# Dense attention of a four-layer network: scores laid out by keys instead of by queries

## The chip, the cores and the metric

The kernel runs on one core of one Trainium2 chip. The metric is the device time of one execution in microseconds (us). The core has five engines that run side by side: TensorE (PE in the profile; its weight loads are shown apart as PEld), VectorE (DVE), ScalarE (ACT), GpSimd (POOL) and SyncE (SP, which issues most transfers). Matrix products are written to eight PSUM banks of 128 partitions and 512 f32 columns; everything else lives in SBUF.

## The reference

The network works on x of 4 batches, 1024 positions and 128 features, in this order: a feed-forward layer, an attention by distances with 16 heads, the feed-forward layer again, a local attention with gated layer, the dense causal attention that this document is about, and the local layer again. What the change touches is the dense attention, 16 heads of 64 features (cut):

```python
xn = (x - mu) / jnp.sqrt(var + 1e-05) * ln_gamma + ln_beta
qkv = jnp.einsum('bnd,ed->bne', xn, w_qkv)
...
q, k, v = (reshape(q) * scale, reshape(k), reshape(v))
sim = jnp.einsum('bhid,bhjd->bhij', q, k)
sim = jnp.where(causal, mask_value, sim)
sim = sim - jax.lax.stop_gradient(jnp.max(sim, axis=-1, keepdims=True))
attn = jax.nn.softmax(sim, axis=-1)
out = jnp.einsum('bhij,bhjd->bhid', attn, v)
out = out.transpose(0, 2, 1, 3).reshape(b, n, INNER)
return jnp.einsum('bne,de->bnd', out, w_out) + b_out
```

The result is added to x.

## The kernel before

**A planner sets the order.** Every piece of work is a small Python function, a step, that is filed with `at(t, f)` under a due time. The steps run once as a recording: each instruction is priced by `cost` (L285), and which step reads or writes which buffer is noted. `order` (L352) then plays the steps through a model of the five engines and of the buffers, takes on each engine the ready step that is most urgent, and `best_order` (L563) repeats this six times, with urgencies taken from the play before, and keeps the shortest. The real instructions are issued in that order, and `follow` (L221) ties each engine to it. So the order on each engine is fixed when the kernel is built, by the prices in `cost`, over all six layers at once. All instructions are issued by one helper, which is why the profile puts them all on line 237. Buffers come from a few large tensors: `wordsP` is PSUM, `wordsS` and `wordsR` are SBUF areas for the whole run (of `WORDS` and `ROUNDED` words a partition, the second for the rounded type fp32r), and `words` is an area of `SWING` words that is given from layer to layer.

For an f32 matmul the price of TensorE is (L292 to L298)

```python
            x, w = args[2], args[1]
            if x.dtype == F32:
                t = 4 * free_size(x) / 2400
```

where `x` is the streaming operand and `w` the weights; 0.004 us are added.

**The dense attention** is `attn1` (L1087). It works through 32 head pairs `n` (4 batches of 8 pairs; a pair is 2 heads of 64 features, 128 rows in all), one every `T` microseconds of due time. For each pair, `project` (L1204) makes queries and keys, features on the partitions and positions in the columns, each split into a rounded high part and a low part so that two passes of the rounded type give the precision of f32 (tiles `q`, `k` and `kz`); `value` (L1255) makes the values with positions on the partitions; `norm` (L1149) does the LayerNorm of the next batch, one tile of 128 positions beside each pair.

`heads` (L1273) then takes a tile `i` of 128 queries. `score` (L1279) puts queries on the partitions and up to 512 keys in the columns of a PSUM bank (banks 0 to 3), two passes with the queries as weights, and adds the causal mask to the diagonal tile by a bf16 matmul. `top` and `top2` take the negated maximum of each row on VectorE, `exp` takes the exponential on ScalarE straight from PSUM with the maximum as its bias and sums each row in its accumulator, `inverse` takes the reciprocal of the sum, and `normalise` (L1316) multiplies the row by it on GpSimd. `turn` (L1320) turns each 128 x 128 tile of exponentials on TensorE, 72 a pair, into banks 4 and 5, and `keep` (L1328) copies them out, two of three on ScalarE and the third on VectorE. `weigh` (L1350) takes two tiles of queries together: for each tile of keys and each head, 64 value columns are the weights, 256 turned exponentials stream, and the two heads write partitions 0 to 63 and 64 to 127 of bank 6. `output`, `project_out` and `collect` add the bias, project and add to x, through bank 7, which projections and values use as well.

Of the kernel before, what the change touches and what calls it, by code (L numbers as in the profile page):

```python
# [19 lines left out]
S = 1024  # L20
# [5 lines left out]
BANKS, ROUNDED, SWING, WORDS = 4096, 14208, 10240, 28744  # L26
# [65 lines left out]
class Plan:  # L92
# [222 lines left out]
    def prepare(self):  # L315
# [25 lines left out]
        for g in self.used_tags:  # L341
            for slot in g.slots:
                for c in slot:
                    c.tags[g] = True

# [6 lines left out]
    def order(self):  # L352
# [69 lines left out]
        def take(s, found):  # L422
            for (t, slot), b in zip(found, s.buffers):
                b.slot, b.lo = slot, slot[0].lo
                for c in slot:
                    c.free = False
                    s.behind += [c.held] if c.held is not None else [x for h in b.tag.before[c] for x in h.buffers]
                b.tag.next += 1
            for b in s.buffers:
                for g in b.slot[0].tags:  # L430
                    wake(g)
# [163 lines left out]
class Macaron:  # L595
# [491 lines left out]
    def attn1(self, ph, T0, lead):  # L1087
# [4 lines left out]
        T = 30.9  # L1092
# [56 lines left out]
        def norm(t0, w, b, t):  # L1149
# [13 lines left out]

            def scale():
                mv, v, y = V[K]
                V["xn", K] = tile_([128, D], "xn", 3)
                ve.tensor_scalar(V["xn", K], x(), mv[:, 0:1], y, ALU.subtract, ALU.mult)
# [20 lines left out]
            self.rsqrt(V, tile_, [t0 + (0.2 + 0.1 * j) * w for j in range(8)], lambda: V[K][1:], K + ("r",))  # L1188
# [8 lines left out]
        low_key = lambda j: plan.tile([128, 512], f"a1.kz{j}", R, FR, swing=True, kept=True)  # L1197
# [55 lines left out]


        def value(t0, b, g, t):  # L1255
            ks = slice(128 * (t % 4), 128 * (t % 4) + 128)

            def start():
                V["v", b, g, t] = tile_([128, 512], f"v{g}{t}")
                h, l = V["h", b, t // 4]  # L1260
                ps = V["pv", b, g, t] = wide()
                pe.matmul(ps, h[:, ks], W["h", 4 + g], start=True, stop=False)
                pe.matmul(ps, h[:, ks], W["l", 4 + g], start=False, stop=False)
                pe.matmul(ps, l[:, ks], W["h", 4 + g], start=False, stop=True)

            def keep():
                ve.tensor_copy(V["v", b, g, t], V["pv", b, g, t])

            at(t0, start)
            at(t0 + 0.8, keep)  # L1270


        def heads(t0, n, i):  # L1273
            TK = 128 * (i + 1)
            parts = [slice(c, min(TK, c + 512)) for c in range(0, TK, 512)]
            two = len(parts) == 2
            K = (n, i)

            def score(z, k):  # L1279
                ks = parts[z]  # L1280
                w = ks.stop - ks.start
                dg = ks.stop == TK
                if z == 0:
                    V["m", K, k] = tile_([128, 3], "nm", 8), tile_([128, 3], "su", 8), tile_([128, 1], "rc", 8)
                q1, k1, kz = V["q", n, i // 4], V["k", n, z], V["kz", n, z]
                qs, ks = slice(128 * (i % 4), 128 * (i % 4) + 128), slice(0, w)
                sc = V["s", K, k, z] = plan.bank("a1.s", [0, 1, 2, 3])
                pe.matmul(sc[:, 0:w], q1[k][:, qs], k1[k][:, ks], start=True, stop=False)
                pe.matmul(sc[:, 0:w], q1[k][:, qs], kz[k][:, ks], start=False, stop=not dg)
                if dg:  # L1290
                    pe.matmul(sc[:, w - 128 : w], self.identb, W["cm"], start=False, stop=True)

            def top(z, k):
                o = V["m", K, k][0][:, z : z + 1]
                ve.tensor_reduce(o, V["s", K, k, z][:, 0 : parts[z].stop - parts[z].start], AX.X, ALU.max, negate=True)

            def top2(k):
                nm = V["m", K, k][0]
                ve.tensor_reduce(nm[:, 2:3], nm[:, 0:2], AX.X, ALU.min)

            def exp(z, k):
                nm, su, _ = V["m", K, k]
                if z == 0:
                    V["e", K, k] = tile_([128, S], "e", 4)
                sc = V["s", K, k, z][:, 0 : parts[z].stop - parts[z].start]
                c = 2 if two else 0
                ac.activation(V["e", K, k][:, parts[z]], sc, AF.Exp, bias=nm[:, c : c + 1], accum_out=su[:, z : z + 1])

            def inverse(k):
                _, su, rc = V["m", K, k]  # L1310
                if two:
                    ve.tensor_reduce(su[:, 2:3], su[:, 0:2], AX.X, ALU.add)
                c = 2 if two else 0
                ve.reciprocal(rc, su[:, c : c + 1])

            def normalise(k):  # L1316
                e = V["e", K, k][:, 0:TK]
                gp.tensor_scalar(e, e, V["m", K, k][2], 1.0, ALU.mult, ALU.mult)

            def turn(k, c):  # L1320
                m = min(4, i + 1 - 4 * c)
                if i % 2 == 0:
                    V["et", n, i // 2, k, c] = tile_([128, 4, 2, 128], "et", 6)
                pt = V["t", K, k, c] = plan.bank("a1.t", [4, 5], (128, 4, 128))
                for j in range(m):
                    pe.transpose(pt[:, j, :], V["e", K, k][:, 128 * (4 * c + j) : 128 * (4 * c + j) + 128], self.ident)

            def keep(k, c, dve):  # L1328
                m = min(4, i + 1 - 4 * c)
                E = ("et", n, i // 2, k, c)  # L1330
                put = ve.tensor_copy if dve else ac.copy
                put(V[E][:, 0:m, i % 2, :], V["t", K, k, c][:, 0:m, :])

            for z in range(len(parts)):
                for k in range(2):
                    at(t0 + 0.45 * z + 0.9 * k, score, z, k)
                    at(t0 + 0.9 * z + 0.9 + 0.1 * k, top, z, k)
                    at(t0 + 2.2 + 0.1 * k + 0.5 * z, exp, z, k)
            for k in range(2):
                if two:  # L1340
                    at(t0 + 2.1 + 0.1 * k, top2, k)
                at(t0 + 3.5 + 0.1 * k, inverse, k)
                at(t0 + 3.6 + 0.1 * k, normalise, k)
                for c in range((i + 4) // 4):
                    at(t0 + 5.0 + 0.1 * k + 0.2 * c, turn, k, c)
                    self.turns = self.turns + 1
                    at(t0 + 5.5 + 0.1 * k + 0.2 * c, keep, k, c, self.turns % 3 == 0)


        def weigh(t0, n, i2):  # L1350
            b, p = divmod(n, 8)
            h = i2 // 2

            def products():
                if i2 % 2 == 0:
                    V["po", n, h] = plan.bank("a1.o", [6])
                po, c = V["po", n, h], 128 * (p % 4)
                c0 = 256 * (i2 % 2)
                for j in range(2 * i2 + 2):
                    u = 128 if j == 2 * i2 + 1 else 0  # L1360
                    for k in range(2):
                        pe.matmul(
                            po[64 * k : 64 * k + 64, c0 + u : c0 + 256],
                            V["v", b, p // 4, j][:, c + 64 * k : c + 64 * k + 64],
                            V["et", n, i2, k, j // 4][:, j % 4].rearrange("p u s -> p (u s)")[:, u:256],
                            start=(j == 0),
                            stop=(j == 2 * i2 + 1),
                            skip_group_check=True,
                        )

            def output():
                V["oT", n, h] = tile_([128, 512], "oT", 2)
                ac.activation(V["oT", n, h], V["po", n, h], AF.Identity, bias=W["bias"][:, 16 + p : 17 + p])
# [11 lines left out]
            at(t0, products)  # L1385
            if i2 % 2:
                at(t0 + 3.5, output)
                at(t0 + 4.5, project_out)
                at(t0 + 5.5, collect)
# [4 lines left out]
        self.turns = 0  # L1394
# [12 lines left out]
        work = [2 * (3.3 * (i + 1) + 2) for i in range(8)]  # L1407
        for n in range(N):
# [11 lines left out]
            for i in range(8):  # L1420
                ti = t0 + T * sum(work[:i]) / sum(work)
                heads(ti, n, i)
                if i % 2:
                    weigh(ti + 7.0 + 0.15 * i, n, i // 2)
# [576 lines left out]
def tile_macaron(ctx: ExitStack, tc: tile.TileContext, a: dict, out: bass.AP, phases=PHASES):  # L2001
# [3 lines left out]
    for k, ph in enumerate(phases):  # L2005
# [3 lines left out]
        elif ph == "attn0":  # L2009
            t = m.attn0(ph, t + 3.0, 46.0)  # L2010
        elif ph == "attn1":
            t = m.attn1(ph, t + 3.0, 40.0)
        else:
            t = m.ffn1(ph, t + 3.0, k == len(phases) - 1)
# [71 lines left out]
```

## Time and profile before

| what | value |
|---|---|
| median of the runs shown | 3249.35 us (3249.25 to 3252.34) |
| the profiled execution | 3244.27 us, of which 3242.3 us are the span from first to last instruction |
| mean granted TensorE clock | 0.984 |
| busy over the span: PE, PEld | 3033.2 us (94%), 2128.3 us (66%) |
| busy over the span: DVE, ACT, POOL | 2237.5 us (69%), 2455.6 us (76%), 1461.8 us (45%) |
| the dense attention in the trace | about 1430 to 2510 us |

How to read it. A line of a group has the engine, the operation, output and inputs by tile names, for matmuls the weights as rows*columns and then the streaming operand as partitions x columns, the type, the number of instructions, their busy time and the mean length of one in ns, and the idle time before them with what ended it. Matmuls are pipelined: the recorded lengths of neighbours overlap, so the cost of one in a stream is the distance between starts and not its length. A line of a timeline has start and length in us of a run of equal instructions.

### The profile page before, as it was taken

The numbers are of one execution on the slowest core, as the hardware profiler recorded it, in microseconds if no ns is written. First come the engines' busy times: TensorE is split into PE (matmuls) and PEld (weight loads), VectorE is DVE, ScalarE is ACT, GpSimd is POOL, SyncE is SP. The second block draws the span as 40 slices with busy tenths as digits, with TensorE's granted clock in tenths as the row PEclk, the third lists the DMA queues.
The fourth block names the chain that finished last, engine by engine and source line by source line (L and its number), as shares of the span: only waits on it lengthen the run. The fifth ranks groups of instructions, "written<-read, shape, count | busy, mean of one in ns | idle before, by whom it ended". The sixth has DMA issues, their size and how long they took to land.

```text
span 3242.3 us, 76442 instructions
## 1 busy us (share of the span) xinstructions
PE 3033.2 (94%) x27033; PEld 2128.3 (66%) x27060; DVE 2237.5 (69%) x6889; ACT 2455.6 (76%) x6818; POOL 1461.8 (45%) x1627
## 2 busy tenths in 40 slices
PE   8999999989998999889999999999999899999988
PEld 6322222667776777667777777777777677777767
DVE  8433341568767676788888888887787787676774
ACT  6999999778868686647767766777777788686873
POOL 1000000179958585433333333333343799585870
PEclk9999999999999999989999999999999999999999
DMA  1000000022212121222222121222231322122211
GB/s 40 1 1 1 1 3 11 25 69 64 55 39 59 44 56 31 52 67 46 47 52 45 42 51 42 45 48 52 45 84 35 75 56 58 37 59 46 57 42 30
DMA packets 212596, 138.96 MB, mean 43 GB/s; under 512 B 148516, under 2 KB 167800, under 8 KB 212216
## 3 DMA queue, kind: packets, MB, share of 16 engines
q1 hardware_dynamic: 211496, 133.51, 18.1%
q8 instruction: 217, 3.56, 0.5%
q14 instruction: 163, 1.34, 0.1%
q0 software_dynamic: 720, 0.56, 0.1%
HBM read 19.22 MB, written 2.10 MB: 7 GB/s over the span
## 4 chain that ended last, share of the span: by engine, by line
PE 54%; DVE 17%; ACT 17%; issue 6%; POOL 5%; DMA 1%; SPq 1%; DVEq 0%; ACTq 0%; POOLq 0%
PE wordsP L237 54%; ACT wordsS L237 12%; DVE wordsS L237 11%; DVE words L237 4%; POOL wordsS L237 4%; ACT words L237 4%; POOL words L237 1%; DVE wordsP L237 1%; DVE wordsR L237 1%; SPq L237 1%; ACT wordsR L237 0%; DMA wordsS<-wordsS 0%; ACT wordsP L237 0%; DMA words<-W_vT 0%; DMA words<-words 0%
## 5 line engine op out<-in xcount | busy, mean ns | idle before, releaser
L237 PE MATMUL wordsP<-wordsS 128*128 128x128 f32 (+7 forms) x12013 | 1653.3, 330 | 131.6 <-POOL wordsS L237 48.7
L237 ACT ACTIVATE wordsS<-wordsP,wordsS 128x128 f32<-128x128 f32 (+4 forms) x1952 | 920.8, 495 | 349.8 <-PE wordsP L237 211.0
L237 PEld LDWEIGHTS wordsP<-wordsS 128*128 128x128 f32 (+3 forms) x10248 | 916.2, 144 | 356.2 <-POOL wordsS L237 101.8
L237 POOL TENSOR_SCALAR wordsS<-wordsS 128x128 f32<-128x128 f32 (+7 forms) x630 | 478.0, 761 | 686.3 <-DVE wordsS L237 489.0
L237 PE MATMUL wordsP<-wordsR 128*128 128x512 f32 (+2 forms) x2592 | 725.9, 411 | 20.1 <-DVE wordsR L237 5.9
L237 POOL TENSOR_TENSOR wordsS<-wordsS 128x512 f32<-128x512 f32 (+1 forms) x518 | 541.5, 1060 | 445.4 <-DVE wordsS L237 422.1
L237 ACT COPY wordsS<-wordsP 128x512 f32<-128x512 f32 (+4 forms) x1040 | 543.2, 540 | 188.1 <-PE wordsP L237 181.0
L237 DVE TENSOR_REDUCE wordsS<-wordsP 128x1 f32<-128x512 f32 (+4 forms) x1024 | 576.4, 581 | 75.3 <-PE wordsP L237 68.8
L237 PE MATMUL wordsP<-wordsS,words 128*64 128x64 f32 (+3 forms) x6216 | 521.3, 298 | 32.3 <-DVE words L237 12.6
L237 PEld LDWEIGHTS wordsP<-wordsR 128*128 128x128 f32 (+1 forms) x2592 | 454.7, 192 | 124.0 <-ACT words L237 10.2
L237 ACT ACTIVATE wordsS<-wordsP 128x1024 f32<-128x1024 f32 (+3 forms) x640 | 515.7, 869 | 25.1 <-PE wordsP L237 20.7
L237 PE MATMUL wordsP<-words 128*128 128x512 f32 (+3 forms) x1540 | 418.1, 376 | 11.9 <-DMA words<-W_vT 10.6
L237 ACT ACTIVATION_READ_ACCUMULATOR wordsS<-wordsP,wordsS 128x1 f32 x1792 | 397.5, 222 | 0.0
L237 DVE COPY wordsS<-wordsP 128x512 f32<-128x512 f32 (+4 forms) x444 | 238.6, 550 | 211.0 <-PE wordsP L237 206.2
L237 PEld LDWEIGHTS <-wordsS 64*128 64x128 bf16 (+1 forms) x1792 | 117.9, 95 | 389.3 <-issue 372.2
L237 PEld LDWEIGHTS wordsP<-wordsS,words 128*64 128x64 f32 (+2 forms) x5704 | 300.4, 136 | 99.1 <-issue 47.5
L237 DVE TENSOR_TENSOR wordsS<-wordsP,wordsS 128x256 f32<-128x256 f32 (+3 forms) x560 | 251.9, 461 | 160.7 <-PE wordsP L237 123.1
L237 DVE TENSOR_TENSOR words<-wordsP,wordsS 128x256 f32<-128x256 f32 (+1 forms) x448 | 227.3, 526 | 129.8 <-PE wordsP L237 83.9
L237 PEld LDWEIGHTS wordsP<-words 128*128 128x128 f32 x1540 | 247.7, 192 | 43.4 <-DMA words<-W_kT 10.6
L237 PEld LDWEIGHTS wordsP<-words,wordsS 64*64 64x64 f32 (+1 forms) x4672 | 186.6, 142 | 78.3 <-issue 54.6
L237 PE MATMUL wordsP<-words,wordsS 64*64 64x128 f32 (+1 forms) x4672 | 227.2, 279 | 7.7 <-POOL words L237 2.7
L237 ACT ACTIVATE words<-wordsP,wordsS 128x512 fp32r<-128x512 f32 (+1 forms) x192 | 131.2, 690 | 73.3 <-PE wordsP L237 66.3
(62 smaller groups left out, 2263.7 us busy)
## 6 DMA issues: line engine op xcount, KB each, us to landing
words<-words SPq DMA_DIRECT2D x648, 128.0 KB
wordsS<-words SPq DMA_DIRECT2D x88, 128.0 KB
wordsS<-wordsS SPq DMA_DIRECT2D x48, 128.0 KB
wordsS<-wordsS SPq DMA_DIRECT2D x48, 112.0 KB
wordsS<-c_rot SPq DMA_DIRECT2D x16, 256.0 KB
wordsS<-L_attn_x SPq DMA_DIRECT2D x8, 256.0 KB
words<-wordsS SPq DMA_DIRECT2D x16, 128.0 KB
out_dram<-wordsS SPq DMA_DIRECT2D x8, 256.0 KB
```

Source lines behind the costliest of these rows:

```text
L237: self.follow(engine, getattr(engine.engine, name)(*args, **kw))
```

## The change

The scores are laid out the other way round. `heads` goes, and `block` takes 512 queries of one head: for each tile `j` of 128 keys it puts the keys on the partitions and the queries in the columns (the keys are now the weights, the queries stream). ScalarE copies each such tile from PSUM to SBUF, and VectorE keeps a running maximum `M` over the tiles, 128 x 512. `M` is turned on TensorE, reduced by VectorE to one maximum for each query, spread again over all partitions by a second turn of a broadcast column, and copied out by ScalarE as `B`. GpSimd subtracts `B` from the stored scores, and ScalarE takes the exponential in place. These tiles already have keys on the partitions, so they go into `weigh` as the weights, in tiles of 128 x 128, and the values stream, with a 65th column of ones whose product is the sum of the exponentials. `divide` divides by it on VectorE, and only the output (four tiles of 128 x 128 for 512 queries of a pair) is turned, for the projection. Beside that: the LayerNorm scales on ScalarE and its root is written out in small VectorE steps; a woken planner step may also be one that waits for a tag sharing the place (`peers`); the low keys move from the swinging area to the rounded one; `T`, area sizes and one due time change; the tile of ones is filled by GpSimd for the first batch.

```diff
-BANKS, ROUNDED, SWING, WORDS = 4096, 14208, 10240, 28744
+BANKS, ROUNDED, SWING, WORDS = 4096, 14208, 7168, 31816
...
+        for g in self.used_tags:
+            g.peers = {h: True for slot in g.slots for c in slot for h in c.tags}
...
-                for g in b.slot[0].tags:
+                for g in b.tag.peers:
                     wake(g)
...
-        T = 30.9
+        T = 29.0
...
             def scale():
-                mv, v, y = V[K]
                 V["xn", K] = tile_([128, D], "xn", 3)
-                ve.tensor_scalar(V["xn", K], x(), mv[:, 0:1], y, ALU.subtract, ALU.mult)
+                ac.activation(V["xn", K], x(), AF.Identity, bias=V["rt", K], scale=V[K][2])
...
-        low_key = lambda j: plan.tile([128, 512], f"a1.kz{j}", R, FR, swing=True, kept=True)
+        low_key = lambda j: plan.tile([128, 512], f"a1.kz{j}", R, FR, kept=True)
...
+        ones = lambda g, t: tile_([128, 8, 65], f"v{g}{t}", 1, F32, False, True)
...
-        def heads(t0, n, i):
...
+        def block(t0, w, n, h, k):
+            K = (n, h, k)
+            b, p = divmod(n, 8)
+            J = 4 * h + 4
+
+            first = [max(0, j - 4 * h) for j in range(J)]
+            groups = [range(j, j + 2) for j in range(0, 4 * h, 2)] + [range(4 * h + z, 4 * h + z + 1 + z // 2) for z in range(3)]
...
+            def score(j):
...
+                ks, c = slice(128 * (j % 4), 128 * (j % 4) + 128), 128 * first[j]
+                q1, k1, kz = V["q", n, h][k][:, c:512], V["k", n, j // 4][k][:, ks], V["kz", n, j // 4][k][:, ks]
+                sc = V["s", K, j] = plan.bank("a1.s", [0, 1, 2])[:, 0 : 512 - c]
+                dg = j >= 4 * h
+                pe.matmul(sc, k1, q1, start=True, stop=False)
+                pe.matmul(sc, kz, q1, start=False, stop=not dg)
                 if dg:
...
+                    pe.matmul(sc[:, 0:128], W["cm"], self.identb, start=False, stop=True)
+
+            def store(j):
+                ac.copy(part([j]), V["s", K, j])
+
+            def top(j):
...
+                ve.tensor_tensor(V["M", K][:, c:512], V["s", K, j], other, ALU.max)
+
+            def turn():
+                pt = V["t", K] = plan.bank("a1.t", [3, 4], (128, 4, 128))
+                for u in range(4):
+                    x = part([0])[:, 0:128] if h == u == 0 else V["M", K][:, 128 * u : 128 * u + 128]
+                    pe.transpose(pt[:, u, :], x, self.ident)
+
+            def top2():
+                V["m", K] = tile_([128, 4], "nm", 3)
+                ve.tensor_reduce(V["m", K], V["t", K], AX.X, ALU.max)
+
+            def spread():
+                pt = V["tb", K] = plan.bank("a1.t", [3, 4], (128, 4, 128))
+                for u in range(4):
+                    pe.transpose(pt[:, u, :], V["m", K][:, u : u + 1].broadcast_to([128, 128]), self.ident)
+
+            def keep():
+                V["B", K] = tile_([128, 4, 128], "B", 3)
+                ac.copy(V["B", K], V["tb", K])
+
+            def shift(q):
+                x, y = part(q), flat(V["B", K])[:, 128 * first[q[0]] : 512]
...
+                gp.tensor_tensor(x, x, y, ALU.subtract)
+
+            def exp(q):
+                ac.activation(part(q), part(q), AF.Exp)
+
+            def weigh(j):
+                if j == 0:
+                    V["po", K] = plan.bank("a1.o", [5, 6])[:, 0:260].rearrange("p (u k) -> p u k", k=65)
+                v = V["v", b, p // 4, j][:, 2 * (p % 4) + k, :]
+                for u in range(first[j], 4):
+                    e = part([j])[:, 128 * (u - first[j]) : 128 * (u - first[j]) + 128]
+
+                    pe.matmul(V["po", K][:, u, :], e, v, start=(j == u == 0), stop=(j == 4 * h + u), skip_group_check=True)
+
+            def divide():
...
+                ve.reciprocal(rc, po[:, :, 64])
+                o = V["on", n, h][:, :, 64 * k : 64 * k + 64]
+                ve.tensor_tensor(o, po[:, :, 0:64], rc.unsqueeze(2).broadcast_to([128, 4, 64]), ALU.mult)
+
+            def turn_o():
+                pt = V["ot", n, h] = wide()
+                for u in range(4):
+                    pe.transpose(pt[:, 128 * u : 128 * u + 128], V["on", n, h][:, u, :], self.ident)
...
-        work = [2 * (3.3 * (i + 1) + 2) for i in range(8)]
+        work = [0.14, 0.14, 0.36, 0.36]
...
+            for j, (h, k) in enumerate(((0, 0), (0, 1), (1, 0), (1, 1))):
+                block(t0 + T * sum(work[:j]), T * work[j], n, h, k)
...
-            t = m.ffn1(ph, t + 3.0, k == len(phases) - 1)
+            t = m.ffn1(ph, t + (3.0 if k < 4 else 8.0), k == len(phases) - 1)
```

More of the change, by code (lines that the diff above doesn't have):

```diff
@@ L1162, in var, with root @@
                 ve.tensor_scalar(v, mv[:, 1:2], 1.0 + EPS, EPS * EPS, ALU.mult, ALU.add)
+            def root(j):
+                mv, v, y = V[K]
+                if j == 0:
+                    V["rt", K] = tile_([128, 1], "rt1", 3)
+                    ve.tensor_scalar(y.bitcast(I32), v.bitcast(I32), -0.5, float(0x5F3759DF), ALU.mult, ALU.add)
+                    return
+                u = V["rt", K]
+                if j in (1, 4):
+                    ve.tensor_scalar(u, y, y, v, ALU.mult, ALU.mult)
+                elif j == 2:
+                    ve.tensor_scalar(u, u, -10.0 / 3.0, u, ALU.add, ALU.mult)
+                elif j == 3:
+                    ve.tensor_scalar(y, u, 5.0, y, ALU.add, ALU.mult)
+                elif j == 5:
+                    ve.tensor_scalar(u, u, -0.5 * 0.375**3, 1.5 * 0.375, ALU.mult, ALU.add)
+                elif j == 6:
+                    ve.tensor_scalar(y, u, y, None, ALU.mult)
+                else:
+                    ve.tensor_scalar(u, mv[:, 0:1], y, -1.0, ALU.mult, ALU.mult)
             def scale():
-                mv, v, y = V[K]
                 V["xn", K] = tile_([128, D], "xn", 3)
-                ve.tensor_scalar(V["xn", K], x(), mv[:, 0:1], y, ALU.subtract, ALU.mult)
+                ac.activation(V["xn", K], x(), AF.Identity, bias=V["rt", K], scale=V[K][2])
             def bias_x():
@@ L1187, in norm @@
             at(t0 + 0.1 * w, var)
-            self.rsqrt(V, tile_, [t0 + (0.2 + 0.1 * j) * w for j in range(8)], lambda: V[K][1:], K + ("r",))
+            for j in range(8):
+                at(t0 + (0.2 + 0.1 * j) * w, root, j)
             at(t0 + 1.1 * w, scale)
@@ L1258, in start @@
             def start():
-                V["v", b, g, t] = tile_([128, 512], f"v{g}{t}")
+                if b:
+                    V["v", b, g, t] = ones(g, t)
                 h, l = V["h", b, t // 4]
@@ L1264, in start, with clear @@
                 pe.matmul(ps, l[:, ks], W["h", 4 + g], start=False, stop=True)
+            def clear():
+                V["v", b, g, t] = ones(g, t)
+                gp.memset(V["v", b, g, t][:, :, 64:65], 1.0)
             def keep():
-                ve.tensor_copy(V["v", b, g, t], V["pv", b, g, t])
+                ve.tensor_copy(V["v", b, g, t][:, :, 0:64], V["pv", b, g, t].rearrange("p (h k) -> p h k", k=64))
+            if not b:
+                at(t0 - 0.1, clear)
             at(t0, start)
@@ L1270, in value @@
             at(t0 + 0.8, keep)
-        def heads(t0, n, i):
[L1274 to L1289, printed above, removed]
-                if dg:
[L1291 to L1347, printed above, removed]
@@ L1350, in weigh, with part @@
[L1350 to L1369, printed above, removed]
+        def block(t0, w, n, h, k):
[4 more added lines that the diff above has]
+            groups = [range(j, j + 2) for j in range(0, 4 * h, 2)] + [range(4 * h + z, 4 * h + z + 1 + z // 2) for z in range(3)]
+            group = {j: q for q in groups for j in q}
+            words = lambda q: 128 * sum(4 - first[j] for j in q)
+            def part(q):
+                lo = words(range(group[q[0]][0], q[0]))
+                return V["st", K, group[q[0]]][:, lo : lo + words(q)]
+            def score(j):
+                q = group[j]
+                if j == q[0]:
+                    V["st", K, q] = tile_([128, words(q)], f"st{words(q) // 128}", {8: 5, 4: 5, 3: 8}[words(q) // 128])
+                plan.await_place(V["st", K, q])
+                ks, c = slice(128 * (j % 4), 128 * (j % 4) + 128), 128 * first[j]
[4 more added lines that the diff above has]
+                pe.matmul(sc, kz, q1, start=False, stop=not dg)
+                if dg:
+                    pe.matmul(sc[:, 0:128], W["cm"], self.identb, start=False, stop=True)
+            def store(j):
+                ac.copy(part([j]), V["s", K, j])
+            def top(j):
+                c = 128 * first[j]
+                if j == 1:
+                    V["M", K] = tile_([128, 512], "M", 3)
+                    other = part([0])[:, c:512]
+                else:
+                    other = V["M", K][:, c:512]
+                ve.tensor_tensor(V["M", K][:, c:512], V["s", K, j], other, ALU.max)
[16 more added lines that the diff above has]
+                x, y = part(q), flat(V["B", K])[:, 128 * first[q[0]] : 512]
+                if len(q) > 1:
+                    x, y = x.rearrange("p (j s) -> p j s", s=512), y.unsqueeze(1).broadcast_to([128, len(q), 512])
+                gp.tensor_tensor(x, x, y, ALU.subtract)
+            def exp(q):
+                ac.activation(part(q), part(q), AF.Exp)
+            def weigh(j):
+                if j == 0:
+                    V["po", K] = plan.bank("a1.o", [5, 6])[:, 0:260].rearrange("p (u k) -> p u k", k=65)
[4 more added lines that the diff above has]
+            def divide():
+                if k == 0:
+                    V["on", n, h] = tile_([128, 4, 128], "on", 2)
+                po, rc = V["po", K], tile_([128, 4], "rc", 3)
+                plan.await_place(V["on", n, h])
+                ve.reciprocal(rc, po[:, :, 64])
[5 more added lines that the diff above has]
+                    pe.transpose(pt[:, 128 * u : 128 * u + 128], V["on", n, h][:, u, :], self.ident)
@@ L1371, in output @@
             def output():
                 V["oT", n, h] = tile_([128, 512], "oT", 2)
-                ac.activation(V["oT", n, h], V["po", n, h], AF.Identity, bias=W["bias"][:, 16 + p : 17 + p])
+                ac.activation(V["oT", n, h], V["ot", n, h], AF.Identity, bias=W["bias"][:, 16 + p : 17 + p])
             def project_out():
@@ L1383, in collect @@
                 ve.tensor_tensor(x, V["pw", n, h], x, ALU.add)
[L1385 to L1389, printed above, removed]
+            for j in range(J):
+                t = t0 + w * j / J
+                at(t, score, j)
+                at(t + 0.5, store, j)
+                if j:
+                    at(t + 0.9, top, j)
+            t = t0 + w + 1.0
+            for f in (turn, top2, spread, keep):
+                at(t, f)
+                t += 0.8
+            for q in groups:
+                for z in ([q] if words(q) == 1024 else [[j] for j in q]):
+                    at(t, shift, z)
+                    t += 1.1 * words(z) / 512
+                at(t, exp, q)
+                for j in q:
+                    at(t + 0.6 + 0.1 * j, weigh, j)
+            t += 1.5
+            at(t, divide)
+            if k:
+                for f in (turn_o, output, project_out, collect):
+                    t += 0.9
+                    at(t, f)
         N = 8 * self.B
         tb = T0 - lead
-        self.turns = 0
         at(tb - 3, load)
@@ L1419, in attn1 @@
                     value(t0 + 10 + 8 * j, (n + 4) // 8, (n + 4) // 4 % 2, 2 * (p % 4) + j)
[L1420 to L1424, printed above, removed]
+            for j, (h, k) in enumerate(((0, 0), (0, 1), (1, 0), (1, 1))):
+                block(t0 + T * sum(work[:j]), T * work[j], n, h, k)
         end = T0 + N * T
```

## The prediction

> **What bounds the kernel now.** I read the page first, then a table of engine times by stage, then the groups of instructions with shapes kept apart in the steady middle of the stage that changes, then short timelines of TensorE, whose rows give the one price that matters. The profiled execution took 3244.27 us (a span of 3242.3 us and 2.0 us around it); the median of the runs shown is 3249.35 us, 5.1 us more, so I sum in the trace and add the difference to that median.
>
> The stage is the dense attention. Its first GpSimd pass over 1024 columns begins at 1445 us and its last at 2508 us, and TensorE has its shapes from about 1430 to 2510 us. Busy time by engine there (PE, weight loads PEld, DVE, ACT, POOL, granted clock):
>
> ```profile
> 1430.00:2510.00 1080.00, 1060.87 (x7867) 810.07 (x7865) 879.68 (x2645) 777.43 (x2231) 393.30 (x533) 1.00 0.22 49
> ```
>
> 1080 us for 32 head pairs is 33.75 us a pair. TensorE is busy for 98%, at full clock; VectorE 81%, ScalarE 72%, GpSimd 36%. The groups from 1600 to 2200 us, 17 pairs, TensorE first:
>
> ```profile
> L237 PE MATMUL wordsP<-wordsS 128*128 128x128 f32 x1533 | 226.3, 276 | 11.6 <-DVE wordsS L237 5.9 <-POOL wordsS L237 3.8 <-DVE words L237 0.7
> L237 PE MATMUL wordsP<-wordsS 128*64 128x256 f32 x1092 | 133.7, 386 | 0.4 <-DVE wordsS L237 0.4
> ...
> L237 DVE TENSOR_REDUCE wordsS<-wordsP 128x1 f32<-128x512 f32 x208 | 139.6, 682 | 24.9 <-PE wordsP L237 22.6 <-issue 0.2
> ...
> L237 ACT COPY wordsS<-wordsP 128x512 f32<-128x512 f32 x138 | 79.5, 588 | 69.5 <-PE wordsP L237 68.8 <-ACT wordsS L237 0.3
> ```
>
> Counts first. The second row is the weighing of the values: the code issues 32 such matmuls a pair, 544 in 17 pairs, and the trace has 1092 records: an f32 matmul is two records, each with a weight load of its own. The first row is 72 turns of exponentials a pair, one of the LayerNorm, and 8 output projections at two records: 89 a pair, 1513 in 17, so a turn is one record. Means are no price here, since matmuls overlap in the pipeline; prices come from spacings in timelines (start, length):
>
> ```profile
> 1653.26 3.18 PE L237 MATMUL wordsP<-wordsS 128*64 128x256 f32 x28
> ...
> 1665.43 4.03 PE L237 MATMUL wordsP<-wordsS 128*128 128x128 f32 x35
> ```
>
> 28 weighing records run two at a time (the two heads of a pair sit in different halves of the array's columns), so these are 14 steps: (3.18 - 0.38) / 13 = 0.215 us a step. 35 turns: (4.03 - 0.28) / 34 = 0.110 us each. Lastly, the row nearest to what the change brings, f32 weights with hardly anything to stream, from the setup of the local attention:
>
> ```profile
> 731.16 0.76 PE L237 MATMUL wordsP<-wordsS,words 128*114 128x1 f32 x6
> ```
> ```profile
> 731.16 0.67 PEld L237 LDWEIGHTS wordsP<-wordsS,words 128*114 128x114 f32 x6 [0.17 <-issue]
> ```
>
> Six records stream one column each and still come about 0.1 us apart: a load lasts 0.18 us, so (0.67 - 0.18) / 5 = 0.098. A record whose stream is short pays for its weight load. It is no floor of a record as such: the page has the weighing loads of 64 columns in the local attention at 5704 loads in 300.4 us, 0.053 each. So the load goes with the columns, and 128 take 0.098 x 128 / 114 = 0.110 us, which is also what a turn takes.
>
> **The change, part by part, for one pair.** *Scores.* Query and key swap their places; 24 blocks of the same widths, two passes each, the same 16 masks. Nothing for TensorE.
>
> *Turns.* 72 turns of exponentials go. Four blocks a pair turn their maxima (16) and spread them (16), and the output is turned (8): 40. Saved: 32 x 0.110 = 3.5 us.
>
> *Weighing.* Out go 32 steps of 0.215 and, for the narrower diagonal ones, 8 at half (an estimate by width): 7.7 us. In come, for each head, 10 products of the upper half of the queries and 26 of the lower: 72 f32 matmuls with 128 exponential columns as weights and 65 value columns streaming, out to 128 partitions, so no two run side by side. 144 records. By the row of one column they are bound by the load: 144 x 0.110 = 15.8 us. The lower bound is the stream alone: a turn streams 128 columns in at most 0.110, so 65 take 0.056, and 144 take 8.1 us. The upper bound is load and stream one after the other, 0.166, 23.9 us; the 35 turns at 0.110 exclude it, since they load and stream as much each and do not take 0.22. I take 15.8. The planner's cost (line 294) is four times the width over 2400, 0.112 us for the whole matmul, half of this; its order packs TensorE on a price that the trace does not bear out.
>
> The TensorE page of the Trainium skill (TensorE: Matmul & The Clock Gate, Back-to-back issue gap) gives about 81 ns for each load and matmul in a stream of 128 columns. By it the 144 records would take 11.7 us, and TensorE would lose 0.5 us a pair instead of 4.6 (an estimate from that page). The same page (LDWEIGHTS, and Weight-path perf modes) says that a load takes the number of columns over 1.2 GHz and that the fast load is not for FP32, which makes 107 ns; the rows here side with that one.
>
> TensorE in sum: -3.5 - 7.7 + 15.8 = +4.6 us a pair, 147 us over 32.
>
> *VectorE.* Out: the maxima of rows, their small joins and reciprocals and a third of the exponential copies, some 22 us a pair. In: 20 maxima from PSUM (0.28 to 0.69 each by the copies of like width, 10.5 us), four reductions of 512 columns (0.682, 2.7 us), four divisions (2.3 us). 27.5 falls to about 20.
>
> *ScalarE.* 24 score blocks are copied out: 12 of 512 at 0.588 and 12 narrower at 0.27 to 0.48, 11.6 us. Exponentials come from SBUF without accumulator reads: 16 instructions over 9216 columns, 9 to 11 us by the rows of the old ones. Spread maxima 2.4, projections and output 4.2, LayerNorm 0.7: 28 to 30 us, from 24.3.
>
> *GpSimd.* The normalising (12 us) goes; 20 subtractions over 9216 columns come. Its two-operand rows elsewhere in the trace are 1099 ns for 512 columns and 463 for 128, so 0.25 each and 1.66 ns a column: 20.3 us, 24 by the slowest rows of 512 (1301 ns).
>
> So all three stay under TensorE's need, and what they do costs nothing as long as TensorE has other blocks to work on. A new wait lies within a block: turn, reduce, spread, copy, subtract, exponential in a row, some 3.5 us before the first weighing. On TensorE's queue the next score blocks stand ahead of that weighing; the wait shows only where they run out.
>
> *What the 33.75 us hold.* Passes of 512 columns start 0.233 us apart in the timeline, and a mask takes 0.127 with the load behind it. So TensorE's records in the stage are 2840 turns and projections at 0.110 (312 us), the weighing (250), 1302 passes of 512 (303), the narrower passes (102) and 512 masks (65), 1032 of the 1080 us. The other 48 us, 1.5 a pair, are waits, mostly for VectorE, which the change relieves. If all of them go, the stage gains 147 - 48 = 99 us in length; if they stay, 147. I take 0.8 us a pair of waits, half of them: +125 us. The ends of the stage (filling, handing over to the local attention) may take 5 us more. Memory moves between pools, sixteen small fills and the planner's wake-ups, which can shuffle other stages, I price at nothing, -10 to +10 us.
>
> Forecast: 3249 + 125 + 5 = about 3380 us.
>
> **The rivals.** *Loads hide.* If a load of 128 columns ran behind the one before, TensorE would need 4.6 - 7.7 = 3.1 us less than now, 32.25 - 3.1 = 29 us a pair, and ScalarE with 28 to 30 us would be next. A pair at 31 us saves 2.75 x 32 = 88 us: 3161. For it: turns do overlap load and stream. Against it: the six records of one column, and seven more such sets in the trace, have nothing to stream and do not come closer. It decides below 0.078 a record, where 144 records cost the 11.2 us saved.
>
> *The chain within a block shows.* If TensorE ran dry at each of four blocks for even 1.5 us (the chain's 3.5 us less what covers it), that is 6 us a pair on top: 3380 + 190 = 3570. For it: three score banks and a copy of 0.588 on each; the planner thinks TensorE cheap, so it may have left too little cover. Against it: TensorE is the engine that falls behind its plan most, so the others are early.
>
> *VectorE was the limit.* In a window of 40 us the chain of waits ran for a third through VectorE. If its relief gave back all waits and the planner's new order another 10 us elsewhere, 3249 + 99 - 10 = 3338. That is the low end of the forecast, not a gain.
>
> **How the numbers follow.** Loads bound and little shows: 0.82. The chain shows: 0.10. Loads hide: 0.08. The forecast's own bounds are 3338 and 3249 + 147 + 5 + 10 = 3411; for records a little over 0.110 (0.120 would add 46 us) and partial waits I go to 3445, and to 3325 below. Faster by over 0.2% (6.5 us, about what a measurement of this kernel can tell from no change) is the rival of hidden loads: 0.08; a result between needs both halves to cancel: 0.02; slower 0.90.
>
> **What would show it.** A group of 128*128 weights with 65 columns, 4608 records, in runs spaced 0.11 us; weight loads busy for nearly the whole stage, where they are 75% now; the stage about 1205 us long; VectorE near 20 us a pair, GpSimd near 21, ScalarE near 28; TensorE's waits small. Wrong would be: a spacing of 0.06 to 0.08 in those runs, or TensorE's idle time going to ScalarE or GpSimd by several us a pair.

## The result, and the profile after

The changed kernel takes 3368.64 us (median; 3364.86 to 3370.32), the one before 3249.30 us: a ratio of 1.0364, 95% interval 1.0346 to 1.0382, 119 us slower. The profiled execution took 3370.32 us with a span of 3368.6 us, 126 us more than the profiled execution before. Two later executions were slow and are left out of their medians: 7078.40 us in the run with the early subtraction and 3652.69 us in the last bf16 run.

First the stage. It now reaches from about 1410 to 2612 us; columns as before (PE, weight loads, DVE, ACT, POOL, granted clock):

```profile
1410.00:2612.00 1202.00, 1176.67 (x8826) 1053.91 (x8825) 752.94 (x1617) 824.03 (x1627) 729.90 (x657) 0.99 0.20 44
```

TensorE is busy for 98% of the stage, as before. Weight loads went from 75% to 88%, VectorE from 81% to 63%, ScalarE from 72% to 69%, GpSimd from 36% to 61%. Before, TensorE was full and VectorE at 81%; now TensorE is full and the others, its weight loads apart, stand below 70%. The groups that answer to those shown of before, again from 1600 to 2200 us (about 15.5 pairs):

```profile
L237 PE MATMUL wordsP<-wordsS 128*128 128x65 f32 x2241 | 282.3, 274 | 0.1
L237 PE MATMUL wordsP<-wordsS 128*128 128x128 f32 x883 | 126.5, 275 | 9.3 <-DVE wordsR L237 7.8 <-DVE wordsS L237 1.5
...
L237 DVE TENSOR_TENSOR wordsS<-wordsP,wordsS 128x512 f32<-128x512 f32 x157 | 107.1, 689 | 91.7 <-PE wordsP L237 55.9 <-ACT wordsS L237 33.1
...
L237 ACT COPY wordsS<-wordsP 128x512 f32<-128x512 f32 x252 | 144.2, 588 | 92.6 <-PE wordsP L237 66.1 <-DVE wordsS L237 25.0
...
L237 POOL TENSOR_TENSOR wordsS<-wordsS 128x1024 f32<-128x1024 f32 x60 | 141.1, 2372 | 162.7 <-ACT wordsS L237 129.0 <-DVE wordsS L237 33.7
```

The new weighing is now TensorE's largest group. VectorE's maxima, ScalarE's copies and GpSimd's subtractions all stand idle before them for a large part of their time, waiting mostly for TensorE or, in a circle, for each other. Then the price in question (start, length). A row of a timeline merges neighbours that share engine, operation and names, also where their shapes differ, and prints the shape of the first; it is not always a run of equal instructions, as it was called above. The first row below is 14 records of the weighing and nothing else. The second is 33 weight loads of 128 f32 columns, 28 of them for the weighing and 5 for neighbours of 128 x 128:

```profile
1809.94 1.67 PE L237 MATMUL wordsP<-wordsS 128*128 128x65 f32 x14
```
```profile
1826.93 3.77 PEld L237 LDWEIGHTS wordsP<-wordsS 128*128 128x128 f32 x33
```

A load lasts 0.184 us, so they start (3.77 - 0.18) / 32 = 0.112 us apart. The 14 records start (1.67 - 0.28) / 13 = 0.107 us apart, with 0.056 for the first distance, behind a long pass, and 0.111 to 0.112 for the rest; over the stage the median of 4021 neighbouring pairs is 0.112. That is what the row of one column had said, scaled to 128. And TensorE's own waits over the stage:

```profile
PE wordsP L237 <- DVE wordsR L237: 8.3, 10, 1.3
PE wordsP L237 <- DVE wordsS L237: 8.1, 10, 3.2
PE wordsP L237 <- ACT wordsS L237: 7.1, 12, 1.5
PE wordsP L237 <- DVE words L237: 0.3, 1, 0.3
```

That is 24 us in the open. More is hidden in gaps between records that still overlap in the pipeline, so this view counts too low; the runs below measure it better.

### The profile page after: what moved, and what is told of

The parts are those of the page before. It is cut to its first block, busy times and chain, and to the rows that moved or that the text cites. A ratio compares the mean times of both kernels' runs of the same rounds, so it can differ in the third digit from the quotient of the medians.

```text
span 3368.6 us, 76173 instructions
## 1 busy us (share of the span) xinstructions
PE 3150.6 (94%) x28056; PEld 2379.6 (71%) x28084; DVE 2095.9 (62%) x5833; ACT 2502.9 (74%) x6210; POOL 1806.3 (54%) x1771
## 4 chain that ended last, share of the span: by engine, by line
PE 57%; ACT 17%; DVE 14%; issue 5%; POOL 4%; SPq 2%; DMA 1%; DVEq 0%; ACTq 0%; POOLq 0%
PE wordsP L237 57%; ACT wordsS L237 13%; DVE wordsS L237 10%; ACT words L237 3%; POOL wordsS L237 3%; SPq L237 2%; DVE wordsR L237 1%; DVE wordsP L237 1%; DVE words L237 1%; POOL words L237 1%; DMA wordsS<-wordsS 1%; ACT wordsR L237 0%; DMA words<-W_kT 0%; ACT wordsP L237 0%; ACT L235 0%
## 5 line engine op out<-in xcount | busy, mean ns | idle before, releaser
L237 PE MATMUL wordsP<-wordsS 128*128 128x65 f32 (+7 forms) x17020 | 2066.1, 313 | 146.5 <-ACT wordsS L237 41.6
L237 POOL TENSOR_TENSOR wordsS<-wordsS 128x512 f32<-128x512 f32 (+4 forms) x1222 | 1349.5, 1129 | 1274.8 <-PE wordsP L237 504.7
L237 PEld LDWEIGHTS wordsP<-wordsS 128*128 128x128 f32 (+3 forms) x15128 | 1377.8, 160 | 299.3 <-issue 89.8
L237 DVE TENSOR_TENSOR wordsS<-wordsP,wordsS 128x512 f32<-128x512 f32 (+4 forms) x1552 | 770.0, 510 | 428.9 <-PE wordsP L237 267.9
L237 ACT COPY wordsS<-wordsP 128x512 f32<-128x512 f32 (+3 forms) x1474 | 753.8, 538 | 323.3 <-PE wordsP L237 201.4
L237 ACT ACTIVATE wordsS<-wordsP,wordsS 128x128 f32<-128x128 f32 (+2 forms) x1200 | 491.7, 436 | 242.4 <-PE wordsP L237 140.2
L237 ACT ACTIVATE wordsS<-wordsS 128x384 f32<-128x384 f32 (+6 forms) x744 | 416.6, 581 | 53.5 <-POOL wordsS L237 35.1
L237 PE MATMUL wordsP<-wordsS,words 128*64 128x64 f32 (+4 forms) x2808 | 303.9, 255 | 27.0 <-POOL words L237 10.4
L237 DVE TENSOR_REDUCE wordsS<-wordsP 128x4 f32<-128x512 f32 x384 | 261.3, 683 | 68.3 <-PE wordsP L237 67.0
L237 PE MATMUL wordsP<-words,wordsR 128*128 128x512 f32 (+3 forms) x768 | 267.3, 348 | 0.0
```

The costliest lines, as they stand in the source:

```text
L237: self.follow(engine, getattr(engine.engine, name)(*args, **kw))
```

## The experiments

Each run is compared with the kernel before on the same chip: 3248 to 3250 us throughout. By "stage" I mean below the time from the first to the last causal-mask matmul of the dense attention: 1091.0 us before, 1203.0 us after. Only the run with the long stream keeps the order of the change on every engine. The others get an order of their own from the planner, and part of each difference may come from that: among the runs below, one buffer fewer moves the stage by 3 us, and another price alone by 31.

**Is it the load?** The stream is made twice as long, and nothing else.

```diff
-                v = V["v", b, p // 4, j][:, 2 * (p % 4) + k, :]
+                c = 65 * (2 * (p % 4) + k)
+                v = flat(V["v", b, p // 4, j])[:, min(c, 392) : min(c, 392) + 128]
```

> The change, with 128 value columns streamed past each tile of exponentials instead of 65 (63 neighbouring columns ride along and their products are not used); planner prices held, so that the order on every engine stays. Theory (the weight load of 128 f32 columns sets the pace, 0.112 us a record, and the stream hides in it): a stream of 128 is 0.107 us and still hides, spacing stays at 0.11 and the time at 3368 us, within 8. Rival (a fixed cost of about 0.058 us a record and the stream on top of it): spacing 0.165, 4608 records, 244 us more: 3612 us.

Measured 3363.07 us, the stage 1196.7 us. Twice the columns cost nothing (neighbouring records still start 0.112 us apart), so the stream lies wholly behind the load; a fixed cost with the stream on top is out by 250 us.

The other way round, shorter loads:

```diff
-        ones = lambda g, t: tile_([128, 8, 65], f"v{g}{t}", 1, F32, False, True)
+        ones = lambda g, t: tile_([128, 8, 65], f"v{g}{t}", 1, BF, False, True)
...
-                ac.activation(part(q), part(q), AF.Exp)
+                V["e", K, q] = tile_([128, words(q)], f"e{words(q) // 128}", {8: 2, 4: 2, 3: 3}[words(q) // 128], BF)
+                ac.activation(V["e", K, q], part(q), AF.Exp)
```

> The change, with exponentials and values rounded to bf16 for the weighing (the exponential writes a bf16 tile of its own; precision is given up), prices of the weighing held. Theory (loads): a bf16 matmul is one record, and its load is shorter; the 72 matmuls of a pair take 4 to 5 us instead of 16.1, TensorE needs about 26 us a pair, and ScalarE with its 26 us and the waits between engines come next: 29 to 31 us a pair, 3080 to 3145 us, less than before the change. Rival (the chain from maxima to exponentials inside a block, or GpSimd, sets the pace at 38 us a pair): it stays above 3300 us.

Measured 3117.74 us, 0.9595 (0.9581 to 0.9609) of the kernel before: 251 us less than the change, with the same layout and the same amounts of work on the other engines. A row of 13 records, all of them weighing, shows the new price:

```profile
1819.82 0.67 PE L237 MATMUL wordsP<-wordsS 128*128 128x65 bf16 x13
```

(0.67 - 0.20) / 12 = 0.039 us a record with one gap of 0.114 in it; the median of 1775 neighbouring pairs in the stage is 0.029. A product is one record instead of two: some 0.03 against 0.22 us. The run shortens the loads and halves the records at once; together with the long stream, which costs nothing, it leaves the f32 records and their loads as the cause of the slowdown.

**Is it the planner's wrong price?**

```diff
-                t = 4 * free_size(x) / 2400
+                t = max(4 * free_size(x) / 2400, 0.22 if free_size(w) == 128 else 0)
```

> The change, with one number of the planner changed: an f32 matmul with 128 weight columns is priced at no less than 0.22 us, what the trace shows for the weighing. Theory (the loads are real work and TensorE is full): the order changes and the time does not by more than 20 us, 3350 to 3375. Rival (the loads would fit, it is the order packed on a price of half that makes TensorE late): a drop by 50 us or more, below 3320.

Measured 3402.11 us, 33 us slower than the change; the stage took 1234.5 us. Both expectations missed: the right price does not bring the time back, but the order it leads to is worse. Neighbouring weighing records start 0.112 us apart here too, so the loads are the same under this order; most of the 31 us in the stage are waits of TensorE, by the count of starts below. Which step of the order brings them I did not follow up.

**Does the chain inside a block show?** First GpSimd's subtraction is left out.

```diff
-                for z in ([q] if words(q) == 1024 else [[j] for j in q]):
-                    at(t, shift, z)
-                    t += 1.1 * words(z) / 512
+                t += 1.1 * words(q) / 512
```

> The change without the subtraction of the maxima on GpSimd: the exponential takes the stored scores as they are; maxima, turns and spreads stay. It leaves out 23 us of GpSimd a pair and a link of the chain inside each block. Theory (TensorE full, GpSimd and the chain hidden): 3345 to 3370 us. Rival (the chain inside a block shows on TensorE by 1.5 us or more a block): 4 x 1.5 x 32 = 190 us less, below 3200; half of it, 3275.

Measured 3307.88 us, 61 us less: neither the theory (nothing) nor the rival at its price (95 us and more). TensorE has no gap left in this run, from 1600 to 2200 us:

```profile
1600.00:2200.00 600.00, 600.00 (x4606) 542.61 (x4605) 387.42 (x899) 434.60 (x844) 7.29 (x16) 1.00 0.20 45
```

Over its whole stage the waits in the open are 1.8 us. So its stage of 1159.2 us is TensorE's bare need in the new layout, in the order of this run, and by the difference the change has 44 us of waits in its stage. Busy time alone would not show this, since records overlap, but the starts agree: compared with the mean distance that the same sequence of two to five shapes has in this run, the starts of the change have 44 to 49 us too much, and those of the run with the other price 71 to 75. Next, the same GpSimd work without the wait for the maxima:

```diff
-                x, y = part(q), flat(V["B", K])[:, 128 * first[q[0]] : 512]
+                x, y = part(q), W["zeros"][:, 128 * first[q[0]] : 512]
```

> The change with the same subtractions on GpSimd, but of a tile of zeros that is there from the start, so that GpSimd does all its work and no longer waits for the maxima to be turned, reduced, spread and copied; those steps stay, and nothing uses them. What is subtracted is zero instead of the maximum. Leaving GpSimd's subtraction out took 61 us off. Theory (it is the chain from the maxima that TensorE feels): most of the 61 us come back here too, 3305 to 3330. Rival (it is GpSimd's own 23 us a pair, in line before each exponential): 3350 to 3370.

Measured 3313.03 us (three executions), the stage 1164.5 us: 56 of the 61 us are back although GpSimd works as long as in the change (745 us in the stage, 730 there). By the starts 5 to 7 us of waits are left. Both runs have orders of their own, but both lose nearly all waits: it is the chain (turn, reduce, spread, copy, and only then subtract) that TensorE feels, and hardly GpSimd's own time. Which link it waits at is harder to see. A stretch of the chain of waits in the trace of the change, and the busy times in its middle (us, PE, weight loads, DVE, ACT, POOL):

```profile
1799.96 13.14 PE wordsP L237 x98
1813.15 0.44 issue
1813.61 0.44 ACT wordsS L237
1814.05 0.04 issue
1814.09 1.19 ACT wordsS L237 x2
1815.30 0.75 DVE wordsS L237 x2
...
1821.24 33.22 PE wordsP L237 x258
```
```profile
1813.15:1821.24 8.09, 7.17 (x48) 5.57 (x46) 6.47 (x12) 6.63 (x14) 2.84 (x2) 1.00 0.17 37
```

TensorE carries the chain for 13 us and then for 33 us; in the 8 us between, ScalarE and VectorE carry it. But TensorE works for 7.2 of these 8 us; it waits once, for 0.86 us at their end, behind two instructions of VectorE that make low keys and are no link of the chain. So this place shows how the engines hold each other up, and not the 44 us. Are buffers what keeps TensorE from running further ahead?

```diff
-                    V["st", K, q] = tile_([128, words(q)], f"st{words(q) // 128}", {8: 5, 4: 5, 3: 8}[words(q) // 128])
+                    V["st", K, q] = tile_([128, words(q)], f"st{words(q) // 128}", {8: 4, 4: 5, 3: 8}[words(q) // 128])
```

> The change with four instead of five buffers for stored scores of 1024 columns. Two are used by each block of the lower half. Theory one (TensorE covers the chain from maxima to exponentials by running ahead, and these buffers limit how far): 30 us or more are lost, above 3395. Theory two (the order of the plan sets the cover, the buffers are enough): within 12 us of 3368.

Measured 3364.67 us. One large buffer fewer costs nothing, so these are not the limit. The order of the steps and the other buffers, the three score banks among them, were not tested and stay possible.

**What were the waits before?** The same is done to the kernel before: maxima off VectorE, then the division off GpSimd too.

```diff
-                    at(t0 + 0.9 * z + 0.9 + 0.1 * k, top, z, k)
...
-                    at(t0 + 2.1 + 0.1 * k, top2, k)
...
-                ac.activation(V["e", K, k][:, parts[z]], sc, AF.Exp, bias=nm[:, c : c + 1], accum_out=su[:, z : z + 1])
+                ac.activation(V["e", K, k][:, parts[z]], sc, AF.Exp, bias=W["zero"], accum_out=su[:, z : z + 1])
```

> The kernel before, without the maxima of the rows and their joins on VectorE; the exponential takes a bias of zero. VectorE loses some 14 us a pair. Theory (TensorE needs 32.3 of the 33.75 us a pair, and waits for VectorE are the rest): a drop of 20 to 48 us, 3200 to 3230, and no more however idle VectorE is. Rival (VectorE and TensorE are equally bounds): a drop beyond 60 us, below 3190.

Measured 3230.30 us, 18 us less and so just short of the 20 expected, the stage 1072.3 us. So taking all maxima off VectorE is worth 19 us in the stage.

```diff
-                at(t0 + 3.6 + 0.1 * k, normalise, k)
```

> The kernel before without the maxima and without the division of the exponentials on GpSimd, so that the turns wait for the exponential alone. Without the maxima alone it took 3230 us and the stage 1072. This gives TensorE's bare need in the old layout. Theory (TensorE needs some 1032 us of the stage): a further 20 to 40 us, 3190 to 3210. Rival (its need is larger than the sum of spacings, about 1060, and most of the waits are gone already): within 15 us of 3230.

Measured 3205.98 us. The stage is 1060.1 us, and TensorE has no gap left:

```profile
1600.00:2200.00 600.00, 600.00 (x4509) 466.14 (x4508) 303.57 (x994) 441.70 (x1274) 6.85 (x15) 1.00 0.22 48
```

By the total the first theory held; by the stage the rival's number, 1060 us, is the right one. That is TensorE's bare need in the old layout, in the order of this run, and by the difference the kernel before had 31 us of waits in its stage, 19 for the maxima and 12 for the division. Here the starts do not agree as well: by the same count the kernel before has 39 to 48 us of waits, for a need of 1043 to 1052 us in its own order.

**Is the new layout good once loads are short?** The kernel before, with a like loss of precision (the normalised exponentials and the values are bf16, and are turned and weighed so):

```diff
-                gp.tensor_scalar(e, e, V["m", K, k][2], 1.0, ALU.mult, ALU.mult)
+                gp.tensor_scalar(V["eb", K, k][:, 0:TK], e, V["m", K, k][2], 1.0, ALU.mult, ALU.mult)
...
-                    V["et", n, i // 2, k, c] = tile_([128, 4, 2, 128], "et", 6)
+                    V["et", n, i // 2, k, c] = tile_([128, 4, 2, 128], "et", 6, BF)
...
```

> The kernel before (scores by queries) with the normalised exponentials and the values rounded to bf16 for turning and weighing; precision is given up as in the bf16 run of the change. TensorE: 72 turns at 0.056 instead of 0.110 and weighing in one pass instead of four, 4 + 5.8 us a pair less, so it needs 23 us. Theory: VectorE with its 27 us and ScalarE with 24 come next, 29 to 31 us a pair, 3110 to 3160: with short loads the two layouts are within 40 us of each other, and what made the change slow was its f32 loads and not its layout. Rival (the layout itself costs): this one is faster than 3070.

Measured 3019.43 us, 0.9293 (0.9279 to 0.9306) of the kernel before and the fastest of all runs here. The rival won: the old layout is 98 us faster than the new one in bf16 (stages 876 and 954.5 us). The first line is the old layout, the second the new one, both in bf16:

```profile
1600.00:2200.00 600.00, 564.37 (x4586) 411.88 (x4584) 560.04 (x1852) 526.68 (x1546) 267.43 (x368) 1.00 0.27 60
```
```profile
1600.00:2200.00 600.00, 528.70 (x4129) 399.82 (x4128) 471.03 (x1049) 496.56 (x1009) 450.67 (x407) 0.98 0.24 54
```

In the old layout TensorE and VectorE are at 94% and 93% and ScalarE at 88%. In the new one nothing is far above 88%: time goes into waits. Taking the subtraction out there as well:

> The change with bf16 weighing and without the subtraction on GpSimd (the exponential takes the stored scores; maxima, turns and spreads stay but are not used). With bf16 the new layout took 3118 us and the old one 3019, and in the new one no engine is above 88%. Theory (the chain through the subtraction is what holds the new layout back once loads are short): about 100 us come off, 3010 to 3050, with ScalarE or TensorE then nearly full. Rival (the layout's own work on ScalarE, copies of all scores and exponentials from SBUF, holds it): it stays above 3080.

Measured 3036.35 us (three executions), the stage 874.8 us. The edit is that of the run without the subtraction, made to the bf16 kernel. 81 us of 98 are back, so with short loads the subtraction is most of what the new layout loses; ScalarE is at 91% then. This run leaves out work that the old layout still does, and whether the chain or GpSimd's own time (75% busy before) costs the 81 us was not separated in bf16.

**And the layers behind?** From the last mask to the end of the last matmul the change takes 751.0 us and the kernel before 732.9.

```diff
-                for g in b.slot[0].tags:
+                for g in b.tag.peers:
```

> The kernel before with the planner's wider wake-up of the change and nothing else of it. After the last mask of the dense attention the changed kernel takes 751 us to its end and the one before 733. If the wake-up shuffles the other layers, this one moves by 5 to 20 us, to 3254 to 3270; if it does nothing there, it stays at 3249, within 4, and the 18 us are from memory, due times or the different neighbours.

Measured 3248.11 us, a ratio of 1.0003 (0.9993 to 1.0012). The wake-up alone does nothing. Without the subtraction, or with it early, the tail is 738 to 739 us. Most of the 18 us are the dense attention's own end: its last weighing record starts 25.2 us behind the last mask in the change, 12.2 us in the kernel before, and 13.7 without the subtraction. About 5 us stay open.

## Why the prediction was right or wrong

The forecast was 3380 us, slower; the time is 3369. The mechanism holds in both directions: doubling the stream is free, shortening the load gives 251 us. But the sum is closer than its terms: three of them were mis-sized in opposite directions, and that the forecast came within 11 us was luck in part.

| term | forecast | measured |
|---|---|---|
| TensorE's bare need in the stage | +147 us | +99 us (1060.1 to 1159.2) |
| TensorE's waits in the stage | -22 us (48 to 26) | +13 us (31 to 44) |
| outside the stage | +5 us | +14 us (-3.5 ahead of it, +17.7 behind it) |
| sum, in the profiled executions | +130 us | +126 us, as the spans differ |

The measured split is that of runs with orders of their own. By the starts, the waits are 39 to 48 us before and 44 to 49 after, so the need grew by 99 to 115 us and the waits by 13 us at most.

*The load* was right: 0.110 forecast, 0.112 measured. The figure of the Trainium skill, about 81 ns for a load and a matmul in a stream (TensorE: Matmul & The Clock Gate, Back-to-back issue gap), is not borne out for f32 here; the row of one column was the better guide.

*Three rows behind it were misread*, since timeline rows and rows with "+2 forms" mix shapes. Of the "35 turns" 32 records are weighing and 3 are 128 x 128; of the "28 weighing records" 24 are. The prices hold all the same, which was luck: in the stage before, 2240 neighbouring pairs of 128 x 128 records start 0.109 us apart, and a full step of the weighing takes 0.216. The 5704 loads are 3328 of 64 columns, 1328 of 128, 1024 of 9 and 24 of 114, and those of 64 start two at a time, 7 ns apart, so this row does not show that a load goes with its columns. Two others do: 0.100 us at 114 columns and 0.112 at 128.

*TensorE's need* was 48 us too high by the runs (32 by the starts at least), 1.5 us a pair. In the two runs without waits, records grouped by kind give for a pair: weighing 8.3 us old (forecast 7.7) and 15.3 us new (15.8), turns and projections 9.9 and 6.2, 3.7 less (3.5), the other products 0.2 less. The old weighing was under-priced mostly in its eight narrower steps, which took 0.16 us each and not half of 0.215; the rest is the first step of a group, 0.267 us, while the 0.215 came from the middle of one. The new one was over-priced: a load behind a long score pass is hidden in part (0.056 us to the next record), and 3 of the 144 records a pair fall beyond the last mask.

*The waits* are the step that failed. I put the 48 us that the spacings left over down mostly to VectorE and gave half of them back. By the runs 31 us were waits, 19 of them for the maxima, and by the starts 39 to 48. VectorE's relief is real, 81% to 63%, but the waits did not shrink: the change has 44 us, and without the waiting for the maxima 38 us of its stage are gone. So the chain inside a block takes VectorE's place. I had that chain as a rival with 0.10 at 190 us: the mechanism was there at a quarter of its price, and it should have stood in the sum rather than beside it. Adding its 44 us to the forecast's waits without seeing the over-priced need would have given 3424 us, still in the range.

*The rival of hidden loads* is excluded by the long stream and by the spacing. *The rival that VectorE was the limit* gave its low end, 3338, by all waits coming back; 3308 was reached only without the subtraction.

*The other engines* stayed off the path in busy time, as said: VectorE 23.5 us a pair (about 20 forecast, though the terms given add up to 21), ScalarE 25.8 (28 to 30), GpSimd 22.8 (20 to 24). What I did not see is that a chain over three of them costs TensorE time although none is full.

## What to carry to other kernels

Price a matmul by its stream and by its load, and take the larger: here f32 records with 128 weight columns started 0.112 us apart with 65 and with 128 columns streaming alike. Swapping which operand is the weight can turn a matmul that was paid by its stream into one that is paid by its load, and a planner that prices the stream alone will like the swap. Look for the row in the trace with the shortest stream to see the load bare, and check that a row holds one shape before you divide by its count. And measure an engine's need by a run in which everything it waits for is left out, knowing that such a run has an order of its own: it gave 1060 us for the kernel before, the starts in its own trace 1043 to 1052, the sum of spacings 1032, and errors of opposite sign hid that in the sum.

## What the runs showed of the hardware that was not expected

A VectorE instruction with two SBUF operands becomes slow beside GpSimd's subtractions. The small product of 128 x 4 from two SBUF tiles, a step of a root, from 1450 to 2450 us; the first line is the change, the second the change without the subtraction:

```profile
L237 DVE TENSOR_TENSOR wordsS<-wordsS 128x4 f32<-128x4 f32 x9 | 10.6, 1183 | 0.2
```
```profile
L237 DVE TENSOR_TENSOR wordsS<-wordsS 128x4 f32<-128x4 f32 x9 | 1.4, 151 | 0.0
```

1183 ns against 151 for four columns. Seven of the nine in the change overlap a subtraction and took 380 to 2292 ns; the other two took 152 and 164. In the kernel before, with its one-operand GpSimd work, eight took 142 to 164 ns and one, beside a GpSimd pass of 1024 columns, 929. The Trainium skill says that the two engines share their SBUF interfaces and contend when a VectorE instruction has two SBUF inputs (GPSIMD Engine Reference, Specifications), and the rows agree. The maxima, whose second operand is in PSUM, took 689 ns in both runs. GpSimd's subtraction of 512 columns took 1281 ns, against the 1099 ns of the group mean in the other layers that the forecast used.
